# A graph layer on one core: part boundaries moved to groups 200 and 330, nine rounds in place of eight, the second table's fill spread over other groups

## The chip, the cores and the metric

The kernel runs on one core of one Trainium2 chip. The metric is the device time of one execution in microseconds; a kernel's time is the median of its runs. A profiled execution has its own time beside them, and the trace belongs to that execution.

## What is computed

One layer of a graph network over 12,500 nodes with 128 features and 412,500 edges (200,000 drawn ones in both directions and one loop per node), sorted by their end node `dst`; `src` is random within that order. Cut to what matters:

```python
h = x @ Wn + bn;  q = x @ Wq + bq;  k = x @ Wk + bk;  v = x @ Wv + bv
eh = edge_attr @ We + be
hmid   = leaky_relu(concat([q[src], k[dst], eh]) @ A1 + b1, 0.2)
scores = leaky_relu(hmid @ A2 + b2, 0.2)                 # 8 heads
w   = softmax(scores.mean(-1), axis=0)                   # one softmax over all edges
out = segment_sum(w[:, None] * v[dst], src, 12500)
y   = layernorm(h + out) * gamma + beta
result = layernorm(x + y)
```

The sums run over `src`, the edges come sorted by `dst`. So the kernel has to bring 412,500 edge records into another order.

## The kernel before

The weights are folded first: A1 is multiplied into Wq, Wk and We, so that a hidden value of an edge is the sum of a q row, a k row and an edge row. Tables of q and h (by node) and of k and v (by node, each split into three bf16 numbers) are written to DRAM while the first groups already run.

**Groups.** The edges form 403 groups of 1024 (8 tiles of 128). For each group (`make`), `rows` expands the k and v rows of a small window of nodes by one-hot matmuls and adds the edge's part (L931, L936), ScalarE copies them out of PSUM as records of 260 numbers (L946, L947: 128 of k plus edge, 128 of v, 4 times the source's number within its block), and GpSimd scatters them to a table in DRAM, one indirect DMA for each tile (L958). The record of an edge goes to the rows of its block: the nodes are dealt over 98 blocks (source modulo 98), and each block has a fixed stretch of rows in the table. VectorE works out the places: one-hots of the blocks (L851), their count (L862), one-hots of the end nodes (L872), places (L900, L911, L913). PE keeps running counts (L880).

**Parts, tables and rounds.** The 403 groups are cut into parts (`PARTS`). Two tables (`rtab`, TABS = 2) are used in turn, so part 2 writes over the table of part 0. Within a part there are stops: at a stop so many tiles of 128 records are certain to be full in each block (4.4 standard deviations are kept back), and a round works through these tiles of all blocks while later groups still scatter. The last round of a part takes what is left. `Plan` works out the tiles of each part and round from the mean number of records and its spread. Before, with ends 165, 307 and 403, the parts have 15, 13 and 9 tiles a block, and the eight rounds 5, 4, 6, then 4, 4, 5, then 4, 5.

**Units.** A round is cut into units of up to three blocks and 15 tiles (`BLK`, `WIDTH`). A unit loads its tiles (L1150), takes the sources out of them (L1177, or L1179 with a mask in the last round of a part), transposes them (L1187, L1194), writes them as a row to DRAM from ScalarE's queue (`put`, L1199) and reads the row back to all partitions on SP's queue (`spread`, L1204), loads the q rows (L1165), and then goes through its tiles in slices of four: one-hots of the sources (`onehot`, L1216, one instruction for each block that a slice touches), transposed records plus q rows in PSUM (`hidden`, L1230, L1239), leaky relu (L1249 on ScalarE, L1253 on VectorE), scores (L1264), heads (L1290). A running reference takes the place of the softmax's maximum (L1300 to L1320), the weights come from one exponential (L1329), and one-hots times weights (`select` L1338, `weigh` L1352) sum the v halves by node (`add`, L1381). From the second round on the block's earlier sum is loaded from DRAM (L1362), scaled and added (L1397); the sum is stored (L1404).

**The order.** It is written out by hand. `sums_of` gives each unit's operations fixed steps (`lags`; `last_lags` for the last round): units of three slices start every 8 steps, in the last round every 6 steps for three slices and every 8 for four. The main loop emits the groups, six positions for each, and between them the steps. `begun` works out by `PACE` at which group each round begins, and the steps of a round are spread evenly from its beginning to that of the next. After the last group the steps still due before the last round are emitted at once, then the last round and the closing (two layer norms, output). In the closing's first part, during the last round, `rows_x`, `moved` and `put_x` copy x plus beta to a table (L1468 on GpSimd).

**Fills.** Rows of a table that no record may reach must hold zeros before a last round reads them. `fill` gives 49 pieces for each of the first two parts, two blocks each. The first table's are written from an SBUF tile before the first stop, the second table's from a DRAM tile of zeros (DRAM to DRAM). Both go through SP's queue (`fill_piece`, L572) at positions spread evenly between two positions of the main loop; the list is emptied from its end.

```python
n1, n2, n3 = 6 * plan.rounds[0][1], 6 * plan.parts[1][0], 6 * G
until = starts[r] + (starts[r + 1] - starts[r]) * (i - 6 * begun[r]) / (
    6 * (begun[r + 1] - begun[r])
)
```

Of the kernel before, what the change touches and what calls it, by code (L numbers as in the profile page):

```python
# [32 lines left out]
ROWS = 3  # L33
XA = 3
SPAN = 42
PARTS = (74, 127, 165), (225, 278, 307), (367, 403)
NP = len(PARTS)
NR = sum(map(len, PARTS))
PACE = 12
TABS = 2  # L40
WIDTH = 15
BLK = 3
# [7 lines left out]
class Plan:  # L50
# [4 lines left out]
    def __init__(self, n, e, nb, groups):  # L55
        self.n, self.e, self.nb, self.groups = n, e, nb, groups
        at = lambda c: groups * c // 403
        ends = [at(part[-1]) for part in PARTS]
        self.parts = list(zip([0] + ends[:-1], ends))

        def means(g0, g1):
            return [
                (min(e, g1 * GT * P) - g0 * GT * P) * max(0, -(-(n - b) // nb)) / n
                for b in range(nb)
            ]
# [22 lines left out]
        for p, (g0, g1) in enumerate(self.parts):  # L88
            t0 = 0
            for g in map(at, PARTS[p][:-1]):  # L90
                t = int(min(m - 4.4 * m**0.5 for m in means(g0, g)) // P) - t0
# [380 lines left out]
def sorted_path(  # L472
# [76 lines left out]
    zeros = dram.tile([P, fmax, WR], FP, name="zeros")  # L549
# [8 lines left out]
    def fill(k, n):  # L558

        b, top = 0, plan.tiles[k]  # L560
        while b < nb:
            m = 1
            while m < n and b + m < nb and plan.fill[k][b + m] == plan.fill[k][b]:
                m += 1
            a = plan.cap // P - plan.fill[k][b]
            if a < top:
                yield b, m, a, top - a
            b += m

    def fill_piece(k, b, m, a, f, source=None):  # L570
        cap = plan.cap
        piece = nc.sync.dma_start(  # L572
            out=rtab[k][b * cap : (b + m) * cap, :]
            .rearrange("(b c) w -> b c w", b=m)[:, a * P : (a + f) * P, :]
            .rearrange("b (p k) w -> p b (k w)", p=P),
            in_=(empty if source is None else source)[:, :f, :]
            .rearrange("p (o k) w -> p o (k w)", o=1)
            .to_broadcast([P, m, f * WR]),
        ).ins
        if k == 0 and source is None:  # L580
            tc.declare_no_dep(piece, group="rows0.0", reason="rows that no record has reached")
            tc.add_to_no_dep_group("fill0", piece)
# [138 lines left out]
    def spans():  # L721

        lim = const.tile([P, 2], FP)
        for i, (op, most) in enumerate(((ALU.max, SPAN - 1.0), (ALU.min, 0.0))):
            nc.vector.tensor_reduce(lim[:, i : i + 1], mm[:, i, :], AX.X, op)
            sign = 1.0 if op == ALU.max else -1.0
            nc.vector.tensor_scalar(
                bad[:, i : i + 1], lim[:, i : i + 1], sign, -sign * most, op0=ALU.mult, op1=ALU.add
            )
# [24 lines left out]
    def far(name, bufs, **k):  # L754
        return making.enter_context(tc.tile_pool(name=name, bufs=bufs, side="right", **k))
# [307 lines left out]
    units = []  # L1063
# [690 lines left out]
    def later():  # L1754

        for c in range(1, len(chunks)):
            yield from edges(tmp, c, CH // 2)
            yield

    def covered():  # L1760

        most = np_.tile([1, G], FP, name="most")
        g = 0
        while g < G:
            h = g
            while h < G and ready.get(h, ng) == ready.get(g, ng):
                h += 1
            nc.vector.memset(most[:, g:h], float(3 * NB * P * ready.get(g, ng) - P))
            g = h
        nc.vector.tensor_tensor(most, start, most, op=ALU.subtract)  # L1770
        nc.vector.tensor_reduce(bad[0:1, 2 + 2 * NR : 3 + 2 * NR], most, AX.X, ALU.max)

    begun, free_at = [], 0
    for p, (_, g, _, t) in enumerate(plan.rounds):
        free_at = max(free_at, g)
        begun.append(free_at)
        free_at += sum(len(bs) * t + 2.7 for q, bs, _ in units if q == p) / PACE

    with tc.manual_schedule():
        n1, n2, n3 = 6 * plan.rounds[0][1], 6 * plan.parts[1][0], 6 * G  # L1780
        n0 = n1 * 9 // 10
        fills = []
        for k, i0, i1, source in (0, 0, 6 * min(plan.gate, plan.rounds[0][1]) - 12, None), (
            1, n1, n2 - 12, zeros
        ):
            pieces = list(fill(k, 2))
            fills += [
                (i0 + (i1 - i0) * j // len(pieces), (k, *piece, source))
                for j, piece in enumerate(pieces)
            ]  # L1790
        fills = fills[::-1]
        tabs, made, nt = tables(), 0, 1 + (2 * ng - 1) * (NB + 7) + ng
        more, sent, ne = later(), 0, 11 * (len(chunks) - 1)
        done, r = 0, 0
        for i, _ in enumerate(_ for p in range(NP) for _ in make(p)):
            while fills and fills[-1][0] <= i:
                fill_piece(*fills.pop()[1])
            while made < nt and made * n0 < i * nt:
                next(tabs, None)
                made += 1  # L1800
            while sent < ne and sent * n0 < i * ne:
                next(more, None)
                sent += 1
            if i == n1:
                for _ in tabs:
                    pass
                for _ in more:
                    pass
                spans()
                covered()  # L1810
                tab_pool.close()
                steps, starts = sums_of(pool("blk", BLKS))
            if i < n1:
                continue
            while r + 1 < NR and i >= 6 * begun[r + 1]:
                r += 1
            if r + 1 < NR:
                until = starts[r] + (starts[r + 1] - starts[r]) * (i - 6 * begun[r]) / (
                    6 * (begun[r + 1] - begun[r])
                )  # L1820
                while done < until:
                    for fn, args in steps[done]:
                        fn(*args)
                    done += 1
        while done < starts[-1]:
            for fn, args in steps[done]:
                fn(*args)
            done += 1
        making.close()
        for name, of, bufs, k in (  # L1830
            ("blk", "blk2", MORE, {}), ("end", "end", 4, {}), ("gamma", "gam", 1, {}),
            ("row", "row2", ROWS, {}), ("ph", "ph2", 2, dict(space=PSUM)),
            ("turn", "trn", 1, dict(space=PSUM)),
        ):
            late[name] = far(of, bufs, **k)
        for step in steps[done:]:
            for fn, args in step:
                fn(*args)


def kernel(tc, n, n_edges, x, xT, src, dst, dst_g, bounds, xN, *rest):
    nc = tc.nc
    plan = Plan(n, n_edges, x.shape[1], src.shape[1] // GT)
    with tc.tile_pool(name="flag", bufs=1) as fpool:
        flag = fpool.tile([1, 1], I32)
        with ExitStack() as ctx:
            sorted_path(ctx, tc, plan, flag, x, xT, src, dst, dst_g, bounds, xN, *rest)
        other = nc.values_load(flag[0:1, 0:1], min_val=0, max_val=1)  # L1848
        with tc.If(other > 0):
            with ExitStack() as ctx:  # L1850
                general(ctx, tc, n_edges, x, xT, src, dst, *rest)
# [60 lines left out]
```

## Time and profile before

| | |
|---|---|
| median of 3 runs | 4864.8 us (4861.4 to 4865.12) |
| profiled execution, its own time | 4862.14 us |
| its span, first to last instruction | 4860.4 us |
| TensorE clock granted, mean | 0.927 |
| busy share PE / VectorE / ScalarE / GpSimd | 83% / 84% / 64% / 68% |
| first scatter starts, last scatter starts (L958) | 59.0 us, 4310.6 us |

In the rows that follow, PE is TensorE's matmul and PEld its weight load, DVE is VectorE, ACT ScalarE, POOL GpSimd, SP SyncE; a trailing q is that engine's queue of DMA issues and waits. L958 is line 958 of the kernel. A group's row has its line, engine, operation, output and inputs with partitions x elements, the count, then busy us and mean ns of one, then the engine's idle time before it and what ended that idle time. A wait's row has the waiting engine and line, what it waited for, the total, how often, and the longest. The ends of matmuls are modelled, so a busy PE is not a PE at its peak.

### The profile page before, as it was taken

To read this page: it belongs to the slowest core of one execution; us is meant where nothing else is said; L and a number is where in the kernel's file an instruction comes from. 1 tells how busy PE (TensorE), PEld (TensorE's weight loads), DVE (VectorE), ACT (ScalarE), POOL (GpSimd) and SP (SyncE) were. 2 spreads that over 40 slices of the span, in tenths; PEclk is the share of its full clock that TensorE was granted. 3 is DMA by queue.
4 is the path that set the end of the run, shared out by engine and by line. 5 is a ranking of instruction groups with operands and counts; after the bars stand their busy time and mean duration, and the time that the engine had idled before them with its cause. 6 is when DMAs were issued, how large, how long until landed. Compare 5 with 4: busy or idle time off the path is not lost. (4 is left out here: it accounts for less than half of the span.)

```text
span 4860.4 us, 84339 instructions
## 1 busy us (share of the span) xinstructions
PE 4017.1 (83%) x26346; PEld 3094.3 (64%) x26626; DVE 4104.8 (84%) x8629; ACT 3110.9 (64%) x8211; POOL 3305.1 (68%) x3280
## 2 busy tenths in 40 slices
PE   3655665688888899999998888899899999998997
PEld 2434443566766666777676666666677777666776
DVE  8878886698888888889898888898999998977877
ACT  2332222477776667777776666676777777777886
POOL 4777777777777767777777777777777777731103
PEclk7777776799999999999999999999999999999999
DMA  6778876999999998999998888999999999989964
GB/s 197 265 252 266 269 266 214 335 358 346 350 338 346 363 337 307 310 321 313 322 313 311 301 295 301 322 338 321 329 337 329 340 322 322 339 286 329 324 222 162
DMA packets 608627, 1484.42 MB, mean 305 GB/s; under 512 B 101632, under 2 KB 309395, under 8 KB 606374
## 3 DMA queue, kind: packets, MB, share of 16 engines
q1 hardware_dynamic: 445822, 1049.05, 64.5%
q0 software_dynamic: 154752, 429.39, 23.2%
q8 instruction: 211, 3.46, 0.3%
q14 instruction: 250, 2.05, 0.1%
q10 hardware_dynamic: 7592, 0.48, 0.1%
HBM read 906.61 MB, written 611.06 MB: 312 GB/s over the span
## 5 line engine op out<-in xcount | busy, mean ns | idle before, releaser
L958 POOL DMA_INDIRECT rtab<-rec,idx x3224 | 3220.9, 999 | 1087.4 <-issue 775.9
L946 ACT ACTIVATE rec<-pkv 128x1024 f32<-128x1024 f32 x806 | 821.7, 1019 | 1090.4 <-DMA rtab<-rec,idx 557.5
L1352 ACT ACTIVATE ohw<-ohs,w 128x128 f32<-128x128 bf16 x3626 | 1187.0, 399 | 70.8 <-DVE ohs L1338 39.0
L1381 PE MATMUL psm<-rt,ohw 128*128 128x128 f32 x7252 | 1020.6, 284 | 3.0 <-ACT ohw L1352 2.5
L1381 PEld LDWEIGHTS psm<-rt,ohw 128*128 128x128 f32 x7252 | 934.6, 196 | 82.2 <-ACT ohw L1352 21.4
L936 PE MATMUL pkv<-WeS,eat 128*128 128x256 f32 x3224 | 932.3, 416 | 0.0
L1253 DVE TENSOR_TENSOR hm<-ph,hm 128x512 f32<-128x512 f32 (+1 forms) x932 | 625.0, 671 | 294.9 <-ACT hm L1249 292.8
L931 PE MATMUL pkv<-kvs,ohd 128*128 128x256 bf16 x3224 | 534.5, 293 | 325.9 <-ACT rec L946 319.6
L931 PEld LDWEIGHTS <-ohd 128*128 128x128 bf16 x3224 | 319.4, 105 | 581.0 <-issue 461.9
L936 PEld LDWEIGHTS pkv<-WeS,eat 128*128 128x128 f32 x3224 | 612.5, 211 | 72.2
L1230 PE MATMUL ph<-ident,rt 128*128 128x128 f32 x3626 | 581.3, 282 | 76.8 <-DVE hm L1253 74.8
L1230 PEld LDWEIGHTS ph<-ident,rt 128*128 128x128 f32 x3626 | 415.2, 145 | 304.5 <-issue 145.5
L1216 DVE TENSOR_SCALAR ohT<-rowB,iotaP,power 128x512 bf16<-128x512 uint8 (+3 forms) x1176 | 577.2, 509 | 30.1 <-DMA rowB<-row 30.0
L1249 ACT ACTIVATE hm<-ph 128x512 f32<-128x512 f32 (+1 forms) x932 | 532.6, 571 | 61.8 <-PE ph L1239 25.4
L872 DVE TENSOR_SCALAR ohd<-dstb,node 128x1152 bf16<-128x1152 uint8 x404 | 565.0, 1399 | 6.1 <-PE pkv L931 6.1
L1239 PE MATMUL ph<-ohT,qs 128*128 128x512 bf16 (+2 forms) x2072 | 495.3, 329 | 41.1 <-DVE ohT L1216 24.0
L900 DVE TENSOR_TENSOR ats<-pc,oh 128x792 f32<-128x792 f32 x403 | 392.0, 973 | 27.5 <-PE pc L880 27.5
L1264 PE MATMUL psc<-hm,A2s 128*32 128x512 f32 (+2 forms) x1864 | 370.1, 607 | 44.7 <-DVE hm L1253 33.7
L862 DVE TENSOR_REDUCE few<-oh 128x99 bf16<-128x792 bf16 x403 | 395.1, 980 | 13.9
L1338 DVE TENSOR_TENSOR ohs<-iotaE,sl 128x512 bf16<-128x512 bf16 (+1 forms) x932 | 395.2, 424 | 5.0 <-ACT ohw L1352 4.8
L911 DVE TENSOR_REDUCE pos<-ats 128x8 f32<-128x792 f32 x403 | 390.5, 969 | 1.9
L1329 ACT ACTIVATE w<-S,ref 128x12 f32<-128x12 f32 (+2 forms) x280 | 84.7, 302 | 340.6 <-DVE ref L1320 327.7
(193 smaller groups left out, 4072.3 us busy)
## 6 DMA issues: line engine op xcount, KB each, us to landing
rt<-rtab SPq DMA_DIRECT2D x177, 1560.0 KB
rt<-rtab SPq DMA_DIRECT2D x96, 1950.0 KB
eat<-in_ea SPq DMA_DIRECT2D x201, 512.0 KB
rtab<-rec,idx POOLq DMA_INDIRECT x3224
dstb<-dtab SPq DMA_DIRECT2D x201, 256.0 KB
qs<-qtab SPq DMA_DIRECT2D x224, 192.0 KB
atab<-old SPq DMA_DIRECT2D x224, 192.0 KB
rtab<-zeros SPq DMA_DIRECT2D x49, 780.0 KB
```

What stands on the lines that cost most here:

```text
L872: nc.vector.tensor_scalar(to, row[:, cols], node, None, op0=ALU.is_equal)
L931: nc.tensor.matmul(pk[:, i, h, :], ohd[t], kvs, start=(h == 0), stop=False,)
L936: nc.tensor.matmul(pk[:, i, :, :D], eat[:, (j + i) * P : (j + i + 1) * P], WeS, start=False, stop=True,)
L946: nc.scalar.activation(rec[:, :, :, : 2 * D], pk, AF.Copy)
L958: one_tile = nc.gpsimd.indirect_dma_start(out=rtab[p % TABS][:, :], out_offset=bass.IndirectOffsetOnAxis(ap=idxs[g][:, t : t + 1], axis=0) ...
L1216: nc.vector.tensor_scalar(st["oh"][k][:, (a - t0) * P : (b - t0) * P], st["rowB"][:, a * P : b * P], iotaP, power[:, bs[u] : bs[u] + 1], o ...
L1230: nc.tensor.matmul(ph[:, j * P : (j + 1) * P], st["rt"][:, t0 + j, :D], ident, is_transpose=True, start=(j == 0), stop=False,)
L1239: nc.tensor.matmul(ph[:, cols], st["qs"][:, j0 // t, s, :], oh[:, cols], start=False, stop=(s == 1 and j1 == t0 + n),)
L1249: nc.scalar.activation(hm, state[i]["ph", k][:, : n * P], AF.Copy, scale=SLOPE)
L1253: nc.vector.tensor_tensor(hm, ph[:, : n * P], hm, op=ALU.max)
L1352: nc.scalar.activation(ohw[:, j, :], ohs[:, :, j], AF.Copy, scale=st["w"][:, t0 + j : t0 + j + 1])
L1381: nc.tensor.matmul(st["psS"][:, (1 + u) * P : (2 + u) * P], ohw[:, j, :], st["rt"][:, t0 + j, D : 2 * D], start=(k == 0), stop=(k == t - 1),)
```

## The change

Four lines in two places change. The parts get 200, 130 and 73 groups in place of 165, 142 and 96, with stops at 74, 127 and 166 in the first, at 260 and 300 in the second and at 377 in the third: nine rounds in place of eight. The pace by which `begun` is worked out changes, in tiles a group and in the extra counted for a unit. The second table's fill runs from position 60 (group 10) to n2 - 48 (group 192) in place of n1 (group 74) to n2 - 12 (group 163), and since it now overlaps the first table's, the list is sorted by position.

```diff
-PARTS = (74, 127, 165), (225, 278, 307), (367, 403)
+PARTS = (74, 127, 166, 200), (260, 300, 330), (377, 403)
...
-PACE = 12
+PACE = 11.2
...
-        free_at += sum(len(bs) * t + 2.7 for q, bs, _ in units if q == p) / PACE
+        free_at += sum(len(bs) * t + 1.2 for q, bs, _ in units if q == p) / PACE
...
-            1, n1, n2 - 12, zeros
+            1, 60, n2 - 48, zeros
...
-        fills = fills[::-1]
+        fills = sorted(fills, key=lambda piece: piece[0])[::-1]
```

## The prediction

> **What bounds the kernel now.** I read the GpSimd timeline first. From group 0 to group 402 it does one thing, the eight scatters of a group's records (L958):
>
> ```profile
> 2599.79 0.96 POOL L958 DMA_INDIRECT rtab<-rec,idx  x1 [0.30 <-issue]
> 2601.06 0.96 POOL L958 DMA_INDIRECT rtab<-rec,idx  x1 [0.31 <-issue]
> 2602.32 0.96 POOL L958 DMA_INDIRECT rtab<-rec,idx  x1 [0.30 <-DVE ohs L1338]
> ```
>
> One starts every 1.265 us even when it waits for nothing, so a group can't take less than 8 x 1.265 = 10.12 us. Then the windows, cut where rounds begin or end. Columns: stretch and its us, then busy us and (instructions) of PE, PEld, DVE, ACT, POOL, then the granted clock, the DMA share and GB/s.
>
> ```profile
> 499.00:864.00 365.00, 203.45 (x749) 139.63 (x747) 264.03 (x451) 95.78 (x158) 279.39 (x282) 0.71 0.73 245
> 864.00:1577.00 713.00, 608.80 (x4207) 478.35 (x4252) 613.37 (x1228) 485.34 (x1268) 544.38 (x552) 0.95 1.00 350
> 1577.00:1868.00 291.00, 260.39 (x1698) 198.21 (x1717) 248.03 (x524) 199.19 (x554) 205.34 (x208) 0.95 0.96 339
> 1868.00:2462.00 594.00, 544.95 (x3741) 419.86 (x3788) 530.00 (x1120) 424.63 (x1180) 443.90 (x449) 0.98 0.92 316
> 2462.00:3009.00 547.00, 467.30 (x3088) 356.08 (x3122) 466.38 (x942) 359.76 (x980) 417.93 (x424) 0.97 0.88 303
> 3009.00:3496.00 487.00, 441.67 (x2939) 333.25 (x2974) 430.34 (x900) 342.19 (x947) 369.55 (x376) 0.98 0.93 326
> 3496.00:3935.00 439.00, 400.32 (x2909) 325.57 (x2938) 414.37 (x891) 345.03 (x913) 336.29 (x338) 0.97 0.95 334
> 3935.00:4310.00 375.00, 346.15 (x2345) 263.33 (x2372) 332.68 (x714) 275.45 (x768) 281.43 (x287) 0.99 0.94 324
> 4310.00:4398.00 88.00, 77.03 (x502) 55.38 (x509) 55.12 (x153) 55.66 (x171) 5.44 (x4) 0.95 0.86 299
> 4398.00:4717.00 319.00, 295.31 (x2345) 238.35 (x2373) 251.61 (x680) 279.82 (x823) 25.12 (x12) 1.00 0.84 288
> 4717.00:4860.00 143.00, 105.17 (x814) 100.11 (x813) 101.71 (x409) 83.44 (x243) 52.27 (x28) 0.91 0.49 184
> ```
>
> POOL's count over eight is the number of groups. Us for one group, by row: 10.35, 10.33 (713/552 x 8), 11.19, 10.58, 10.32, 10.36, 10.39, 10.45. So up to 4310 us **GpSimd's issue paces the kernel**, some 2 to 4% over its floor, except from 1577 to 2462. Rounds (the work on finished tiles) run under it nearly free until something else fills up: VectorE is at 414.37/439 = 0.944 in the fifth-from-last row (five-tile units), and the DMA engines are at 1.00 between 864 and 1577. After 4310 the scatters are over and what is left runs alone: 88 + 319 + 143 = 550 us, which is the **tail**. Its middle part is the last round:
>
> ```profile
> L1329 ACT ACTIVATE w<-S,ref x41: 298/307/309, 4315.2 to 4717.3; 128x15 f32<-128x15 f32 x32, 128x12 f32<-128x12 f32 x7, 128x8 f32<-128x8 f32 x1, 128x10 f32<-128x10 f32 x1
> ```
>
> 41 units pass their softmax weights (L1329) there, 8 of the round before (3 blocks of 4 tiles) and 33 of the last. From the first of those 33 (at 4398) to the last (4717) are 32 unit times: 319/32 = 9.97 us for 15 tiles.
>
> The slow stretch from 1577 has its cause in the waits of 1411 to 1826:
>
> ```profile
> DVE sl L1177 <- DMA rt<-rtab: 24.3, 12, 5.6
> ```
>
> A unit's tiles come late, just after the stretch in which 350 GB/s filled the DMA engines. The fill of the second table runs from group 74 to 163, that is on top of the rounds.
>
> **What changes in the counts.** By the formulas of Plan the parts have 18, 12 and 7 tiles a block instead of 15, 13 and 9. The sum stays 37, so 3626 tiles are loaded and worked through either way. Rounds by tiles a block: 5, 4, 6 | 4, 4, 5 | 4, 5 before, and 5, 4, 3, 6 | 4, 3, 5 | 3, 4 after. Units grow from 280 to 313: three rounds now have units of 3 blocks x 3 tiles. The last round has 33 units of 12 tiles instead of 15, and `last_lags` spaces them 6 steps apart instead of 8. So 98 tiles leave the tail, and the price is 33 more units under the scatters.
>
> **VectorE's price of a nine-tile unit.** No nine-tile unit is in the trace; I build it from these groups (count, busy us, mean ns):
>
> ```profile
> L1253 DVE TENSOR_TENSOR hm<-ph,hm 128x512 f32<-128x512 f32 x833 | 570.9, 685 | 278.0 <-ACT hm L1249 276.1
> L872 DVE TENSOR_SCALAR ohd<-dstb,node 128x1152 bf16<-128x1152 uint8 x402 | 564.1, 1403 | 6.1 <-PE pkv L931 6.1
> L862 DVE TENSOR_REDUCE few<-oh 128x99 bf16<-128x792 bf16 x403 | 395.1, 980 | 13.9
> L900 DVE TENSOR_TENSOR ats<-pc,oh 128x792 f32<-128x792 f32 x403 | 392.0, 973 | 27.5 <-PE pc L880 27.5
> L911 DVE TENSOR_REDUCE pos<-ats 128x8 f32<-128x792 f32 x403 | 390.5, 969 | 1.9
> L1338 DVE TENSOR_TENSOR ohs<-iotaE,sl 128x512 bf16<-128x512 bf16 x833 | 349.4, 419 | 2.6 <-ACT ohw L1352 2.4
> L1216 DVE TENSOR_SCALAR ohT<-rowB,iotaP,power 128x512 bf16<-128x512 uint8 x589 | 326.8, 555 | 30.1 <-DMA rowB<-row 30.0
> L851 DVE TENSOR_TENSOR oh<-blk,iotaE 128x792 bf16<-128x792 bf16 x403 | 226.9, 563 | 0.0
> ...
> L1216 DVE TENSOR_SCALAR ohT<-rowB,iotaP,power 128x256 bf16<-128x256 uint8 x293 | 113.6, 429 | 0.0
> L1216 DVE TENSOR_SCALAR ohT<-rowB,iotaP,power 128x384 bf16<-128x384 uint8 x195 | 96.5, 495 | 0.0
> ...
> L1253 DVE TENSOR_TENSOR hm<-ph,hm 128x384 f32<-128x384 f32 x96 | 52.8, 550 | 16.8 <-ACT hm L1249 16.7
> L1216 DVE TENSOR_SCALAR ohT<-rowB,iotaP,power 128x128 bf16<-128x128 uint8 x99 | 49.5, 500 | 0.0
> L1338 DVE TENSOR_TENSOR ohs<-iotaE,sl 128x384 bf16<-128x384 bf16 x96 | 45.0, 468 | 2.4 <-ACT ohw L1352 2.4
> ```
>
> Neighbours overlap; in the timeline the one at 3606.92 lasts 0.68 and the next starts after 0.60:
>
> ```profile
> 3606.92 0.68 DVE L1253 TENSOR_TENSOR hm<-ph,hm 128x512 f32<-128x512 f32 x1
> 3607.52 0.96 DVE L911 TENSOR_REDUCE pos<-ats 128x8 f32<-128x792 f32 x1
> ```
>
> So 0.08 us comes off each. A group's own five: 1.403 + 0.980 + 0.973 + 0.969 + 0.563 - 5 x 0.08 = 4.49 us. In the window 3496 to 3935 are 338/8 = 42.25 groups and, by the three-tile slices, 29 units of 15:
>
> ```profile
> L1253 DVE TENSOR_TENSOR hm<-ph,hm 128x512 f32<-128x512 f32 x86 | 58.6, 682 | 10.6 <-ACT hm L1249 10.5
> ...
> L1253 DVE TENSOR_TENSOR hm<-ph,hm 128x384 f32<-128x384 f32 x29 | 16.0, 550 | 3.7 <-ACT hm L1249 3.7
> ```
>
> (414.4 - 42.25 x 4.49)/29 = 7.75 us for a unit of 15, short instructions included. A nine-tile unit is cut into slices of 4, 4 and 1. Its one-hots (L1216, split where a block ends) are 384, 128, 256, 256 and 128 wide: 2.35 us against 2.90 for the six of a 15. Its L1253 are two of 0.685 and a narrow one, about 0.28 by the step from 512 to 384: 1.65 against 2.60. Its L1338 are two of 0.419 and a narrow one that no row has; between 0 and 0.468 I take 0.25: 1.09 against 1.73. Three instructions fewer give 0.24 of overlap back. Sum: 7.75 - 0.55 - 0.95 - 0.64 + 0.24 = **5.85 us**, 0.65 a tile against 0.52.
>
> **Under the scatters, round by round** (`begun` worked out with PACE 11.2 and 1.2 gives the units per group):
> - Groups 300 to 330, 33 units of nine, 1.10 a group: 4.49 + 6.44 = 10.93 us of VectorE a group. Groups 377 to 403, 1.107 a group: 10.97. Both lie over the 10.37 and 10.45 of today. If VectorE were full they cost 17 + 13 = 30 us more; at today's 0.944 they cost 36 + 30 = 66. I take 0.98, since 14.3 of the 24.6 idle us of that window are the two ScalarE waits shown, which vanish behind a full VectorE: 30 x (11.15 - 10.37) + 25.7 x (11.19 - 10.45) = **+42**.
> - Groups 166 to 200, 0.97 units of nine a group: 10.16, at 0.98 10.4, where today's mean is 10.63; I take 10.6, **-1** (-10 to +5).
> - Groups 143 to 166, today 11.19: the second fill (98 blocks x 3 tiles x 133 KB = 39.1 MB) is spread over 182 groups instead of 89, so 0.21 MB a group leave the stretch. To 10.4: 23 x 0.79 = **-18** (-20 to 0).
> - Groups 200 to 260 take the six-tile round that groups 167 to 227 have now: 34 groups go from 10.32 to 10.58, **+9** (0 to +9).
> - Groups 330 to 377, 0.698 units of 15 a group: 9.90, at 0.944 10.49; **+3** (-5 to +5).
> - Groups 10 to 74 get 13.8 MB of the second fill and 7.2 more of the first (98 x 4 tiles, 52.2 MB against 45.0). At 350 GB/s these 21 MB take 60 us of DMA time; the row 499 to 864 alone leaves 27% of 365 us free, and scatters go on at 10.35: **+2** (0 to +8).
>
> Cost under the scatters: 42 - 1 - 18 + 9 + 3 + 2 = **+37** (-35 to +93).
>
> A rule bears on the nine-tile price. The Trainium skill, Perfetto Trace Analysis, Optimizing Scalar/DVE Operations, puts VectorE's fixed overhead per instruction on SBUF at about 60 ns of engine time. By that, two more splits cost 0.12 us; these rows have 2.35 against 9/12 x 3 x 0.555 = 1.25, less two overlaps 0.94 us more. The trace doesn't agree (429 ns at 256 wide, 555 at 512), and I go by the rows; by the rule a unit would be 5.03 us, both stages would need about 10.05, and the 42 would fall away.
>
> **The tail.** 88 us to the first weights of the last round: 8 units of twelve and a gap of 15 steps become 10 units of nine and 8 steps. A unit takes between 5.85 (VectorE) and 7.9 us (63/8, the same step); 7.0 gives 70 + 8 = 78, **-10** (+8 to -22). Then 32 unit times. If all goes with tiles, 12/15 x 9.97 = 7.98. If bytes rule, a unit has 1.60 + 0.59 + 0.20 MB instead of 2.00 + 0.59 + 0.25, and the 13.8 MB of `rows_x` and `put_x` stay (0.42 a unit): 2.81/3.26, so 8.59. These two rows say that bytes rule first and ScalarE later:
>
> ```profile
> 4398.00:4600.00 202.00, 182.86 (x1432) 144.88 (x1450) 162.44 (x419) 170.35 (x500) 25.12 (x12) 1.00 0.94 330
> 4600.00:4717.00 117.00, 112.45 (x916) 93.48 (x925) 89.17 (x262) 109.47 (x324) 0.00 (x0) 1.00 0.66 215
> ```
>
> The middle, 8.28, saves **54** (44 to 64). The closing 143 us lose a shorter last unit, **-2**. Tail: **-66** (-36 to -90).
>
> **Sum.** Profiled execution 4862.1 + 37 - 66 = 4833; the median of the runs is 2.7 above that execution, so **4836 us**; with the bounds of the terms, that case alone runs from 4790 to 4860.
>
> **Rivals.**
> - *The nine-tile units hide.* Their splits cost only the fixed part, GpSimd paces all 403 groups: 4836 - 42 = **4794**. For: scatters still ran at 10.39 with VectorE at 0.944. Against: 10.9 us don't fit in 10.4 by the rows. The skill's rule above would make it so. Chance 0.20.
> - *The round trip of the source row paces nine-tile units: slower.* `put` writes the transposed sources to DRAM, `spread` reads them back, and SP holds everything behind it, loads included, until the row has landed:
>
> ```profile
> SPq L1204 <- DMA row<-slT: 1918.3, 277, 13.0
> ```
>
>   6.9 us a unit. A unit is 8 steps of the order, whatever its tiles: 12 to 15 us now, 0.91 groups = 9.4 us then; tiles must land 5 steps after their load, 5.9 us instead of 7.9. With all 94 nine-tile units before the last scatter at 11.0 us: 33 x 1.57 + 28.4 x 1.56 = 96 in place of 42, sum 4836 + 54 = **4890**. It ends above today's time from a unit time of about 10.6. Against: the last round does 8 steps in 9.97 us. Chance 0.15.
> - *The tail stays with the DMA engines.* 8.59 a unit and no shorter lead-in: it saves 36, and the 37 above eat it: 4836 + 30 = **4866**. For: 0.94 at 330 GB/s. Chance 0.13.
>
> **Chances and range.** A measurement of this kernel tells about 0.2% (9.7 us). My forecast 0.52 and the first rival are faster: 0.72. The third rival is the same: 0.13. The second is slower: 0.15. The range goes from below the first rival to near the second: 4785 to 4885.
>
> **What would show it.** POOL's last scatter at about 4350 us instead of 4311 and some 485 us after it; VectorE above 0.95 in groups 300 to 330 and 377 to 403 with over 11 us a group; groups 143 to 166 near 10.4 and no L1177 waits for tiles there; units of the last round at 8.0 to 8.6 us. I am wrong on the price if those two stages stay at 10.4, and on the cover if VectorE idles there behind L1204's row or late tiles.

## The result, and the profile after

The changed kernel takes 5032.6 us (median of 4 runs, 5023.95 to 5036.18), the kernel before on the same chip 4863.7 us (4 runs): ratio 1.0345, 95% interval 1.0327 to 1.0363. It is slower by 3.5%, where 4836 us was predicted; the time lies outside the range too. The profiled execution has 5023.95 us of its own, a span of 5022.0 us and a mean granted clock of 0.929, hardly another clock than before (0.927).

The windows of the changed kernel, cut where its rounds begin or end (columns as before: stretch and its us, busy us and instructions of PE, PEld, DVE, ACT, POOL, granted clock, DMA share, GB/s):

```profile
864.00:1577.00 713.00, 609.18 (x4269) 480.39 (x4270) 615.02 (x1232) 490.56 (x1284) 544.59 (x550) 0.96 0.95 329
1577.00:1835.00 258.00, 230.34 (x1551) 175.56 (x1549) 222.00 (x472) 177.98 (x497) 183.11 (x187) 0.97 0.97 338
1835.00:2240.00 405.00, 352.53 (x2411) 275.17 (x2409) 345.89 (x827) 273.64 (x769) 268.61 (x272) 0.95 0.91 301
2240.00:2873.00 633.00, 581.95 (x4037) 446.77 (x4038) 566.96 (x1210) 453.00 (x1256) 475.88 (x481) 0.98 0.91 316
2873.00:3299.00 426.00, 387.30 (x2656) 294.07 (x2654) 379.22 (x794) 305.82 (x852) 316.11 (x320) 0.99 0.94 326
3299.00:3688.00 389.00, 337.90 (x2342) 263.97 (x2342) 326.76 (x804) 265.17 (x753) 239.60 (x241) 0.96 0.86 283
3688.00:4179.00 491.00, 443.59 (x3238) 354.97 (x3239) 459.41 (x995) 378.64 (x1005) 370.68 (x376) 0.98 0.96 334
4179.00:4517.00 338.00, 296.29 (x2092) 232.71 (x2090) 281.35 (x709) 238.27 (x675) 206.75 (x208) 0.97 0.84 275
```

The rows from 1835, 3299 and 4179 are the three stages with nine-tile units (groups 166 to 200, 300 to 330, 377 to 403). POOL's count over eight gives the groups: 34, 30.1 and 26, so 11.9, 12.9 and 13.0 us a group, where the other rows of this table stand at 10.4 to 11.0. And in these three **nothing is full**: in the middle one PE is busy for 0.87 of the time, VectorE 0.84, ScalarE 0.68, the DMA engines 0.86, and GpSimd scatters 8 x 1.265 = 10.12 us of every 12.9.

The difference to before, by the starts of the scatters (L958) of the same groups in the two profiled executions, with two later runs that are told of below:

| stretch | before, us | after | e17, old part ends | e18, slices of three |
|---|---|---|---|---|
| start to group 143 | 1577.1 | +2.4 | +3.6 | +3.3 |
| 143 to 166 | 259.0 | -3.8 | -2.4 | -3.9 |
| **166 to 200** | 361.8 | **+43.6** | -1.6 | **+28.3** |
| 200 to 260 | 626.3 | +6.2 | -3.4 | -0.3 |
| 260 to 300 | 411.9 | +14.5 | -0.2 | +19.5 |
| **300 to 330** | 312.9 | **+75.7** | +6.6 | **+53.9** |
| 330 to 377 | 488.4 | +3.2 | -0.1 | -0.3 |
| **377 to last scatter** | 273.2 | **+63.6** | +11.9 | **+52.4** |
| tail, after the start of the last scatter | 549.8 | -43.8 | -9.8 | -44.4 |
| sum | 4860.4 | +161.6 | +4.6 | +108.5 |

The tail gave 44 us, as it should. Under the scatters 205 us were lost, 183 of them in the three nine-tile stages. (The profiled execution of e18 is the slowest of its four runs, 17 us over their median, so its column shows a little less than the median gains.) The waits of 3310 to 3680, inside the middle one (waiting engine and line, what it waited for, total, times, longest):

```profile
ACT w L1329 <- DVE ref L1320: 72.4, 29, 5.9
POOL rtab L958 <- issue: 55.4, 181, 0.6
DVE hm L1253 <- ACT hm L1249: 48.2, 38, 2.1
POOL rtab L958 <- ACT rec L947: 41.8, 20, 4.3
PEld psm L1311 <- DVE mx L1305: 30.9, 18, 3.1
ACT rec L946 <- PE pkv L936: 29.4, 13, 3.4
```

The same groups in the kernel before (3235 to 3548):

```profile
ACT w L1329 <- DVE ref L1320: 30.4, 16, 4.5
DVE hm L1253 <- ACT hm L1249: 17.9, 19, 3.2
PEld psm L1311 <- DVE mx L1305: 11.4, 12, 2.3
```

ScalarE waits for VectorE (72 us of 370, before 30 of 313), VectorE for ScalarE (48, before 18), PE for VectorE (31, before 11), ScalarE for PE (29), and GpSimd at last for ScalarE's records (42). Each has idle time, and each waits for the next; the first three waits were there before and have more than doubled. The timeline shows how one such wait makes another:

```profile
3509.22 0.28 DVE L1319 TENSOR_REDUCE m<-psm 128x1 f32<-128x128 f32 x1
3509.54 0.16 DVE L1320 SCALAR_TENSOR_TENSOR ref<-m,ref 128x1 f32<-128x1 f32 x1
3509.62 0.78 DVE L1216 TENSOR_SCALAR ohT<-rowB,iotaP,power 128x256 bf16<-128x256 uint8 x2
3509.74 0.30 ACT L1329 ACTIVATE w<-S,ref 128x9 f32<-128x9 f32 x1 [1.75 <-DVE ref L1320]
...
3510.13 0.70 PE L1239 MATMUL ph<-ohT,qs 128*128 128x256 bf16 x4 [0.64 <-DVE ohT L1216]
...
3510.16 1.31 ACT L1352 ACTIVATE ohw<-ohs,w 128x128 f32<-128x128 bf16 x4
...
3511.38 1.04 ACT L1278 ACTIVATE z<-psc,b_c 64x512 f32<-64x512 f32 x2
...
3512.44 0.60 ACT L1249 ACTIVATE hm<-ph 128x512 f32<-128x512 f32 x1
...
3513.07 0.69 DVE L1253 TENSOR_TENSOR hm<-ph,hm 128x512 f32<-128x512 f32 x1 [1.80 <-ACT hm L1249]
```

ScalarE stands 1.75 us at L1329 until VectorE has the reference. Behind it in ScalarE's own order are the weighing (L1352), the relu of the scores (L1278) and then L1249, which doesn't need the reference at all: the matmuls that it reads (L1239) had ended by 3510.83 at the latest, and it starts at 3512.44. VectorE's L1253 needs that L1249, and so VectorE stands 1.80 us. The time that VectorE loses so puts off the references after it. This is one passage; the totals above say that it is common (29 times at L1329 and 38 at L1253, in the time of some 31 units).

After the last scatter the same is to be seen without a group beside it. The rows of the lead-in to the last round (what is left of the nine-tile units), and of the last round up to its last weights:

```profile
4517.00:4603.90 86.90, 78.96 (x491) 56.91 (x490) 55.19 (x174) 56.20 (x176) 2.07 (x1) 0.88 0.77 269
4603.90:4880.00 276.10, 265.35 (x1830) 195.52 (x1831) 199.93 (x526) 210.25 (x655) 27.45 (x13) 0.99 0.82 290
```

and the waits of 4517 to 4604:

```profile
ACT w L1329 <- DVE ref L1320: 25.2, 9, 3.8
DVE hm L1253 <- ACT hm L1249: 18.3, 16, 2.7
```

Last scatter 4516.0, first weights of the last round 4607.1: 91 us, where the kernel before needed 87. The weights of the nine-tile units follow one another at 9.1 us there (4513.5 to 4595.1, nine times), with VectorE busy for 0.64 of the row. Last weights at 4883.3: 276.2/32 = 8.63 us a unit in the last round.

### The profile page after: what moved, and what is told of

It is laid out like the page before. It is cut to its first block, busy times and chain, and to the rows that moved or that the text cites. A ratio compares the mean times of both kernels' runs of the same rounds, so it can differ in the third digit from the quotient of the medians.

```text
span 5022.0 us, 87787 instructions
## 1 busy us (share of the span) xinstructions
PE 4157.7 (83%) x27509; PEld 3201.2 (64%) x27509; DVE 4219.1 (84%) x9220; ACT 3194.7 (64%) x8540; POOL 3310.3 (66%) x3281
## 5 line engine op out<-in xcount | busy, mean ns | idle before, releaser
L958 POOL DMA_INDIRECT rtab<-rec,idx x3224 | 3225.7, 1001 | 1287.8 <-issue 780.9
L1352 ACT ACTIVATE ohw<-ohs,w 128x128 f32<-128x128 bf16 x3626 | 1193.5, 399 | 79.2 <-DVE ohs L1338 39.6
L1381 PE MATMUL psm<-rt,ohw 128*128 128x128 f32 x7252 | 1039.9, 285 | 3.6 <-ACT ohw L1352 3.4
L1381 PEld LDWEIGHTS psm<-rt,ohw 128*128 128x128 f32 x7252 | 942.7, 196 | 83.8 <-ACT ohw L1352 11.9
L1253 DVE TENSOR_TENSOR hm<-ph,hm 128x512 f32<-128x512 f32 (+2 forms) x997 | 635.3, 637 | 322.0 <-ACT hm L1249 320.7
L1230 PE MATMUL ph<-ident,rt 128*128 128x128 f32 x3626 | 593.2, 283 | 91.8 <-DVE hm L1253 90.1
L1216 DVE TENSOR_SCALAR ohT<-rowB,iotaP,power 128x512 bf16<-128x512 uint8 (+3 forms) x1371 | 621.4, 476 | 40.9 <-DMA rowB<-row 40.8
L1239 PE MATMUL ph<-ohT,qs 128*128 128x256 bf16 (+3 forms) x2742 | 569.3, 311 | 39.0 <-DVE ohT L1216 37.9
L1249 ACT ACTIVATE hm<-ph 128x512 f32<-128x512 f32 (+2 forms) x997 | 541.7, 543 | 49.8 <-PE ph L1239 23.3
L1264 PE MATMUL psc<-hm,A2s 128*32 128x512 f32 (+3 forms) x1994 | 407.5, 578 | 48.5 <-DVE hm L1253 40.7
L1338 DVE TENSOR_TENSOR ohs<-iotaE,sl 128x512 bf16<-128x512 bf16 (+2 forms) x997 | 424.1, 425 | 1.1 <-ACT ohw L1352 1.1
L1329 ACT ACTIVATE w<-S,ref 128x12 f32<-128x12 f32 (+3 forms) x313 | 94.6, 302 | 499.3 <-DVE ref L1320 487.7
L862 DVE TENSOR_REDUCE few<-oh 128x99 bf16<-128x792 bf16 x403 | 395.1, 980 | 13.9
```

What stands on the lines that cost most here:

```text
L958: one_tile = nc.gpsimd.indirect_dma_start(out=rtab[p % TABS][:, :], out_offset=bass.IndirectOffsetOnAxis(ap=idxs[g][:, t : t + 1], axis=0) ...
L1216: nc.vector.tensor_scalar(st["oh"][k][:, (a - t0) * P : (b - t0) * P], st["rowB"][:, a * P : b * P], iotaP, power[:, bs[u] : bs[u] + 1], o ...
L1230: nc.tensor.matmul(ph[:, j * P : (j + 1) * P], st["rt"][:, t0 + j, :D], ident, is_transpose=True, start=(j == 0), stop=False,)
L1239: nc.tensor.matmul(ph[:, cols], st["qs"][:, j0 // t, s, :], oh[:, cols], start=False, stop=(s == 1 and j1 == t0 + n),)
L1249: nc.scalar.activation(hm, state[i]["ph", k][:, : n * P], AF.Copy, scale=SLOPE)
L1253: nc.vector.tensor_tensor(hm, ph[:, : n * P], hm, op=ALU.max)
```

## The experiments

Theories, as the expectations name them. **V**, the prediction's: VectorE's work sets the nine-tile stages. **S**: a step of the order takes its time (1.47 us), and a unit has eight, whatever its tiles. **U**: a unit has its own chain of some 12 us. **R**: the source row's round trip. **W**: the unit's work passes back and forth between VectorE and ScalarE (and PE), so that all of them idle.

The first sixteen runs fell on chips where the kernel before takes 5799 to 5907 us (the changed kernel's page of one of them, e14, has a clock of 0.867 and 259 GB/s instead of 0.929 and 301); numbers are therefore only compared with the kernel before on the same chip. A nine-tile stage weighs less there, since from group 74 on no stage goes much under 13 us a group in any kernel. Twenty runs of the kernel before on one such chip lie between 5787.7 and 5835.5 us, so where a single run is set against a single run, a difference below some 50 us says little. The last two runs fell on a chip with 4861 us.

**The part ends alone.** The old ends, everything else as changed (new pace, new fill).

```diff
-PARTS = (74, 127, 166, 200), (260, 300, 330), (377, 403)
+PARTS = (74, 127, 165), (225, 278, 307), (367, 403)
```

> The changed kernel with the parts and stops of before, that is, only the pace and the second table's fill are changed. If the whole loss comes with the nine-tile rounds: within 0.3% of the kernel before, and the groups 143 to 166 tell whether the thinner fill speeds them up (the prediction had 18 us) or not.

5786.7 us (8 runs) against 5811.3 (20): 0.9953 [0.9928, 0.9977], where the changed kernel itself, e14 on that chip, has 1.006.

> The changed kernel as it is, on the same chip, as the base of the two doublings. On a chip like the last four: some 50 us above the kernel before, nine-tile stages at 14 to 15 us a group. On a chip that gives 4864 for the kernel before: 5032, within 10, and 11.9 to 13.0 us a group there.

5848.3 us (8 runs): 1.006 [1.0038, 1.0082].

> The changed kernel with the part ends of before, so no unit of nine tiles; the pace and the second fill stay changed. If the nine-tile rounds carry the whole loss, this is level with the kernel before on its chip or up to 0.5% faster (e13_parts_undone was at 0.9953 on another chip): 0.994 to 1.001 of it. If the new pace or the fill carry a share of the loss, it is over 1.005. Where the kernel before takes about 4864 us, groups 143 to 166 tell what the thinner fill is worth without the new rounds: 11.0 to 11.2 us a group before; 10.4 by the prediction, about 11.1 if the fill is not what slows them.

4864.6 us (10 runs) against 4861.1 (13): **1.0004 [0.9989, 1.0020]**. So the new part ends carry the whole loss, and pace and fill together are worth nothing that can be told from zero where the kernel takes 4861 us. In the table the column of e17 is small in every stretch; the +11.9 before the last scatter and the -9.8 of the tail nearly cancel. Groups 143 to 166 took 256.6 us, 11.16 a group, with about half the fill for each group (49 pieces over 182 groups instead of 89): the fill is not the main thing that slows them.

**Slices of three.** Units of nine (and six) tiles are cut 3, 3, 3 instead of 4, 4, 1.

```diff
-return min(4, m), [(j, min(4, m - j)) for j in range(0, m, 4)]
+s = 3 if m in (6, 9) else 4
+return min(s, m), [(j, min(s, m - j)) for j in range(0, m, s)]
...
```

(The same in the two other places where slices of four are cut.)

> The changed kernel with the units of nine tiles cut into slices of 3, 3 and 3 tiles instead of 4, 4 and 1, still in 8 steps. A slice then is one block, so a unit has three one-hots on VectorE instead of five; VectorE's work for a unit falls by about 0.7 us. Theory V: the three stages fall by about 0.7 us a group, the time to about 4965. Theories S, U and R: the steps and the chain are the same, 5024 with up to 15 less.

5805.5 us, +7 on the kernel before (one run).

> The same kernel as in the run with slices of three, on another chip, since the first chip gave the kernel before itself 5799 us and so blurs every stage. On a chip that gives 4864 for the kernel before. Theory V (VectorE's work): the three stages fall by about 0.7 us a group, the time to about 4965. Theories S, U and R: 5024 with up to 15 less. The first chip speaks for more than V: with slices of three the nine-tile stages ran at 13.5 us a group like all others, with the row three steps earlier at 15.9; if it is the slices' shape that counts, all three stages come to 10.4 to 11 and the time to about 4850.

5909.8, +3 (one run).

> Slices of 3, 3 and 3 alone, as twice before, in the hope of a chip on which the kernel before runs at 4864 us. Theory V (VectorE's work, 0.7 us less a unit): the three stages at 12.2 us a group, the time about 4965. Theory S: 5024. If the shape of the slices is the whole cause, as the two slow chips have it (13.4 to 14.2 us a group against 13.2 in the other stages): 10.4 to 11.2 a group, about 4850.

5939.9, +38 (one run). Of these three single runs none tells V from the others.

> The changed kernel as it is, beside the kernel before on the same chip, as the base for the variants, since three chips in a row gave the kernel before 5799 to 5907 us in place of 4864. On such a chip all stages run at about 13.2 us a group; the three nine-tile stages are expected at 15.6 to 16 us a group, as in the run with the row three steps earlier, and the time 150 to 180 us above the kernel before. On a chip that gives 4864: 5032, within 10.

The changed kernel again, beside the next one: 5928.7 (2 runs), 1.0088 [1.0059, 1.0118].

> Slices of 3, 3 and 3 on the same chip. If the shape of the slices is the larger part of the loss: 100 us or more below the changed kernel, within 40 us of the kernel before, the nine-tile stages within 1 us a group of their neighbours. If VectorE's work alone counts (0.7 us a unit): 50 to 60 us below the changed kernel. Theories S, U and R: no more than 15 below.

5903.5 (5 runs), 1.0050 [1.0032, 1.0068].

> Slices of 3, 3 and 3 in nine-tile units, once more beside the kernel before. On a chip that gives 4864 for the kernel before: theory W (the stages pass back and forth between VectorE and ScalarE; this shape takes about 0.7 us of VectorE's and 0.5 us of ScalarE's work from a unit) 1.0 us or more a unit less, the three stages at 10.9 to 11.9 us a group, the time 4900 to 4960; theory V 4965; theory S 5024. On a chip that gives 5800 to 5900 for it: 20 to 40 us above the kernel before.

5909.8 (8 runs), 1.0028 [1.0002, 1.0054].

> The changed kernel with nine-tile units cut into slices of 3, 3 and 3. If the third, one-tile slice carries most of the loss, this is within 0.5% of the kernel before and its nine-tile stages fall below the 11.7 to 13.1 us a group of the changed kernel. If a unit takes its time whatever its slices, stages 300 to 330 and 377 to 403 stay at about 13 us where the kernel before takes about 4864 us, and the whole at 1.02 or more; where the kernel before takes 5800 to 5900 us, 1.003 to 1.007 as in the runs so far.

4953.7 us (4 runs) against 4861.1 (13): **1.0185 [1.0154, 1.0216]**. So 3, 3, 3 takes back about half of the loss (3.45% to 1.85%), and the other half stays with evenly cut units too; that is between the two forecasts. U, and S and R in the form that the expectations give them (same steps, same chain, at most 15 us less), fall with the 79 us between 5032.6 and 4953.7. Windows of the three nine-tile stages of e18:

```profile
1835.00:2225.00 390.00, 332.97 (x2231) 252.61 (x2231) 336.94 (x769) 255.13 (x742) 267.43 (x272) 0.96 0.93 312
3283.00:3650.00 367.00, 315.41 (x2163) 241.32 (x2162) 318.67 (x745) 246.83 (x724) 235.98 (x241) 0.97 0.89 300
4138.00:4464.00 326.00, 282.03 (x1934) 216.62 (x1931) 272.74 (x654) 222.19 (x651) 205.25 (x208) 0.95 0.86 284
```

In groups 300 to 330 VectorE's work falls from 326.76/30.1 = 10.85 us a group to 10.58, and the group from 12.9 to 12.2: less work by 0.27, less time by 0.7. V can't say why, for VectorE's use is only 0.87 here (0.84 before). V's forecast of 4965 us is close to the time by luck: it came from 0.7 us less of VectorE's work for each unit. In the same rows ScalarE's work falls by 0.61 us a group (265.17/30.1 to 246.83/30.1) and PE's by 0.75, so the run doesn't single out one engine. The waits of 3290 to 3640 of e18 (its lines are one higher from L1264 on):

```profile
ACT w L1330 <- DVE ref L1321: 58.4, 28, 4.7
...
POOL rtab L958 <- ACT rec L947: 32.4, 27, 3.9
...
DVE hm L1253 <- ACT hm L1249: 18.3, 30, 2.0
...
DVE sl L1177 <- DMA rt<-rtab: 16.0, 11, 4.0
```

VectorE's wait for L1249 falls from 48 to 18 us, and a new one appears: for a unit's late tiles (L1177) 16.0 us, where the window of the changed kernel has 0.3. So part of what the even slices free is lost again to the loads. Three rows bear on the first, the relu of the scores ahead of it on ScalarE, in the changed kernel two pieces of which the second has one tile, in e18 one:

```profile
L1278 ACT ACTIVATE z<-psc,b_c 64x512 f32<-64x512 f32 x30 | 20.0, 666 | 2.0 <-PE psc L1264 2.0
...
L1278 ACT ACTIVATE z<-psc,b_c 32x128 f32<-32x128 f32 x28 | 10.0, 358 | 0.3
```

```profile
L1279 ACT ACTIVATE z<-psc,b_c 96x384 f32<-96x384 f32 x28 | 15.7, 560 | 0.0
```

1.02 us against 0.56, between a late reference and the L1249 that VectorE waits for. That this piece is the whole of the gain isn't shown; the one-hots (three instead of five) and the matmuls of the scores change too.

**ScalarE's work or VectorE's, doubled.** In nine-tile units one operation is issued twice: L1278 on ScalarE (1.02 us a unit more) or L1338 on VectorE (2 x 0.417 + 0.442 = 1.28 us a unit more, by its rows in the changed kernel, 3310 to 3680):

```profile
L1338 DVE TENSOR_TENSOR ohs<-iotaE,sl 128x512 bf16<-128x512 bf16 x67 | 27.9, 417 | 0.0
...
L1338 DVE TENSOR_TENSOR ohs<-iotaE,sl 128x128 bf16<-128x128 bf16 x27 | 11.9, 442 | 0.0
```

ScalarE's first:

```diff
-for p0, p1, n in pieces:
+for p0, p1, n in pieces * (2 if units[i][2] == 3 else 1):
```

> The changed kernel with one piece of ScalarE's work done twice in units of nine tiles: the relu of the scores (L1278, 1.0 us a unit in two pieces) is written a second time with the same values. Theory W (in the nine-tile stages the loop passes back and forth between VectorE and ScalarE, neither of them full): a large part of it lands on the stages, 0.5 us or more of 1.0 a unit, 45 to 95 us in all 94 units. Theory V (VectorE's work sets the pace): below 15 us, ScalarE is idle a third of the time.

5902.7 us (2 runs): +54 on the changed kernel (e14), that is 0.55 us for each of 99 units. The interval against the kernel before is wide, 1.0071 to 1.0248. Then VectorE's:

```diff
+for _ in range(2 if units[i][2] == 3 else 1):
     nc.vector.tensor_tensor(ohs[:, :, :n], iotaE[:, :, :n],
     ...
```

> The changed kernel with one piece of VectorE's work done twice in units of nine tiles: the one-hots of L1338 (about 1.0 us a unit, three instructions) are written a second time with the same values. Theories V and W: 45 to 95 us more. If only the steps count (S): below 15 us.

5861.4 us (7 runs): +13 on e14, 0.13 us a unit. Against e14's profiled execution, e11's is 57 us longer, with +60 in the three nine-tile stages, and e12's 15 us longer, with +18 there. By V the VectorE work would count in full and ScalarE's not at all; it is rather the other way round. ScalarE, idle for a third of the stage, is on the path, as W has it; but W expected 45 to 95 us from VectorE's work too, and there it missed: 1.28 us more a unit fit almost wholly into VectorE's idle time. On this chip, with its stages at 13 us a group and more, that is only an indication for the other.

**Fewer steps a unit.** Nine-tile units start every six steps instead of every eight.

```diff
-every=max(8, L), lead=turn + 8, sources=-turn - 2 - e, turn=-turn,
+every=6 if plan.rounds[p][3] == 3 else max(8, L), lead=turn + 8, sources=-turn - 2 - e, turn=-turn,
```

> The changed kernel with one thing altered: units of nine tiles start every 6 steps of the order instead of every 8; their instructions, lags and tiles are the same, and each of the three stages then has 5.8 to 6.6 steps a group instead of 7.8 to 8.9. Theory S (a step costs about 1.47 us of time whatever it holds, because instructions that depend on each other stand one step apart on different engines): the stages at groups 166 to 200, 300 to 330 and 377 to 403 fall from 12.0, 13.0 and 13.0 us a group to 10.4 to 11.0, and the time to about 4850 (4830 to 4880). Theory U (a unit's own chain takes 12 us whatever its steps): 5024, within 10. Theory V, that of the prediction's sum (VectorE's work): 5024, the work is the same. Theory R, the prediction's slower rival (the source row's round trip, 8 steps long): falls too, as under S.

5886.5 us, +88 (one run).

> The same kernel as in the run with nine-tile units every 6 steps, on another chip. Theory S (a step costs 1.47 us whatever it holds): the three stages at 10.4 to 11.0 us a group, the time about 4850 (4830 to 4880). Theory U (a unit's chain of 12 us): 5024, within 10. The first chip lies between: 14.7 against 15.9 us a group.

6020.4, +114 (one run).

> Nine-tile units every 6 steps, once more. On a chip that gives 4864 for the kernel before: theory S about 4850 to 4900, the three stages below 11.5 us a group; theory W 5024, within 20, since no work is taken away. On a chip that gives 5800 to 5900 for it: 60 to 115 us above the kernel before, as twice before.

6000.6 (2 runs), 1.0153 [1.0102, 1.0204]. About twice the loss of the changed kernel on such chips (1.006 to 1.009). S expected a gain; the nine-tile stages of the three runs took 14.1 to 15.6 us a group where the changed kernel on such chips (e14, e9) has 13.6 to 14.5. What gets worse is the hold of buffers: SP's loads of tiles (L1150) wait twice as long until the last sums (L1381) of the unit that used the buffer are done. SP's waits over the whole kernel, in the changed kernel (e14), then in e1:

```profile
SPq L1150 <- PE psm L1381: 88.6, 30, 8.5
```

```profile
SPq L1150 <- PE psm L1381: 180.0, 56, 10.4
```

Behind a waiting load SP holds everything else, the groups' loads too. That this is the whole cause wasn't tried.

**More steps a unit, on the kernel before.** The round that begins at the stop of group 278, with units of 12 tiles, gets 11 steps a unit.

```diff
-every=max(8, L), lead=turn + 8, sources=-turn - 2 - e, turn=-turn,
+every=11 if p == 4 else max(8, L), lead=turn + 8, sources=-turn - 2 - e, turn=-turn,
```

> The kernel before, with the units of one round (four tiles a block, groups 278 to 318) started every 11 steps instead of every 8: 9.0 steps a group with no instruction added. Theory S: these 40 groups go from 10.35 to about 13.3 us, the time to about 4980. Theory U: units are as many as before, the time stays at 4864, within 10. Theory V: 4864, the work is the same. Theory R: as S, its 8 steps must last as long.

5822.0 us, +23 (one run), its stage (groups 278 to 318) at 13.9 to 14.0 us a group, where e1, e3 and e4 of that chip have 13.0 to 13.2 in groups 278 to 300. S expected +115 on a chip with 4864 us. Here the run **doesn't decide**: by S the groups would take 9.0 x 1.47 = 13.2 us, which is what that chip's groups take anyhow. What speaks against one fixed price of a step are traces of the other chips: with the same eight steps a nine-tile unit takes 11.8 us in the changed kernel and 11.1 in e18 (12.9/1.10 and 12.2/1.10), and 9.1 where no group runs beside it.

**The source row three steps earlier.**

```diff
-turn = 11 if nk > 3 else 12
+turn = 15 if plan.rounds[p][3] == 3 else 11 if nk > 3 else 12
```

> The changed kernel with the source row of nine-tile units read, transposed, written and read back three steps earlier (and the load three steps earlier with it), so that the round trip has 11 steps until the one-hots instead of 8; all else is the same. Theory R: a unit's time falls from 12 to about 9 to 10 us, the three stages to 11.2 or less, the time to about 4900 or below. Theory S, U and V: 5024, within 15.

5973.4 us, +175 (one run), the slowest of its chip. R expected a gain; a longer lead holds the six record buffers longer, and L1150's wait for L1381 is 182.2 us here. So R isn't refuted by this run alone. Against R speak the waits where the kernel takes 4861 to 5033 us. SP stands at the row for 214.0 of the 370 us of 3310 to 3680, and for 178.4 of the 313 us of the same groups before (3235 to 3548), the same share; VectorE waits for the row only 40.8 us in the whole changed kernel. The changed kernel, SP's row of that window and VectorE's of the whole, then the kernel before:

```profile
SPq L1204 <- DMA row<-slT: 214.0, 32, 8.3
...
DVE ohT L1216 <- DMA rowB<-row: 40.8, 32, 4.9
```

```profile
SPq L1204 <- DMA row<-slT: 178.4, 23, 11.8
```

**Three changes together**: slices of three, every six steps, and the second fill over by group 72.

```diff
...
-            1, 60, n2 - 48, zeros
+            1, 60, n1 - 12, zeros
```

> The changed kernel with three things altered, each read from its own groups: nine-tile units in slices of 3, 3 and 3; the same units every 6 steps instead of 8; the second table's fill over by group 72, before the first round (it ran to group 192). Shape and spacing are read from groups 300 to 330 and 377 to 403 against the run with the slices alone: Theory S expects a clear fall by the spacing, theories U and V none. The fill is read from groups 143 to 166: if the fill made them slow (11.0 to 11.5 us a group in both kernels), they come to 10.4, some 20 us in all; if not, they stay, and groups 10 to 74 show what the earlier fill costs. On a chip that gives 4864 for the kernel before, S and V together: about 4830; V alone: about 4850.

5936.3 us, +34 (one run). Groups 143 to 166 took 13.40 us each, where e14 and e13 have 13.24 and 13.44: with no fill at all in that stretch it is no faster. The early fill cost groups 10 to 74 nothing there (12.14 us each; e9 and e10 have 12.07 and 12.17).

No run is faster than both kernels wherever it ran: the old part ends with the new pace and fill gain 0.5% on one chip and nothing on the other.

## Why the prediction was wrong

**The cover: VectorE's use of 0.98. This step failed.** "I take 0.98, since 14.3 of the 24.6 idle us of that window are the two ScalarE waits shown, which vanish behind a full VectorE." They didn't vanish, they grew: L1253's waits for L1249 went from 14.3 us in 439 to 48.2 in 370, and they are one half of the loop that the timeline shows. The prediction's own sign for a wrong cover, VectorE idle behind L1204's row or late tiles, was not it: late tiles cost VectorE 0.3 us of that window and the row none. VectorE's use fell from 0.944 to 0.84 and 0.83, and the two stages cost 76 + 64 = 139 us instead of 42. Both bounds of that term (30 and 66; the -35 of the sum takes it at nothing, as the first rival does) assumed a use no lower than in the row of 15-tile units; the use was the unknown, and nothing bounded it from below. The row that it was taken from had 29 units in 42 groups, 0.69 a group, and already left VectorE idle for 0.056 of the time; the nine-tile stages have 1.1 units a group.

**The price itself was right.** VectorE's work: predicted 10.93, 10.97 and 10.16 us a group for the three stages, measured 326.76/30.1 = 10.85, 281.35/26 = 10.82 and 345.89/34 = 10.17. That the parts add up so well is partly luck: the narrow L1338 was too low (0.25 taken, 0.442 in the row above) and the two one-hots of 128 (L1216) too high (0.500 each taken, 0.361 measured in 3310 to 3680).

The rule of the Trainium skill, Perfetto Trace Analysis, Optimizing Scalar/DVE Operations, by which a unit would be 5.03 us, isn't borne out: by it the stage's VectorE work would be near 10.05 us a group, an estimate from the page's 60 ns, where the window has 10.85.

**Groups 166 to 200** were taken as -1, since 10.16 us of VectorE lie under the 10.6 of today: +44. It is the same step: with 0.97 units of nine a group the use went to 345.89/405 = 0.85. Likewise groups 260 to 300, which weren't given a term (0.82 units of twelve a group): +14.5, at a use of 0.89. It can't be the one-tile slice there, for e18 has +19.5.

**The unit's time.** The lead-in to the last round was to have units of 5.85 to 7.9 us, "7.0". With the groups gone and VectorE at 0.64 they took 9.1. A nine-tile unit that runs without groups doesn't go by its VectorE work either; the lead-in gave +4 instead of -10. The upper end was counted wrongly. In the kernel before, the first and the last of the eight units of that stretch pass their weights at

```profile
4315.19 0.30 ACT L1329 ACTIVATE w<-S,ref 128x12 f32<-128x12 f32 x1 [4.01 <-DVE ref L1320]
...
4378.32 0.30 ACT L1329 ACTIVATE w<-S,ref 128x8 f32<-128x8 f32 x1 [0.93 <-DVE ref L1320]
```

and these 63 us are seven intervals, not eight: 9.0 us a unit in eight steps, with 12 tiles (the last has 8) as with nine. In e18 the lead-in has 90.5 us (4463.5 to 4554.0): even slices bring nothing there.

**Groups 143 to 166**: -18 by 0.21 MB a group less fill; it came to -4, and -2.4 in e17. The DMA share of the stretch before did fall, from 1.00 to 0.95, and the L1177 waits of 1411 to 1826 only from 24.3 to 20.5 us. The full DMA engines and the late tiles were seen rightly; that they paced the stretch was a step too far. What paces it isn't settled: L1329 waits in 1580 to 1835 for 30.1 us before and 34.1 in e17.

Of the signs that were named, the last scatter came at 4516 instead of 4350, 506 us after it instead of 485, and VectorE at 0.84 instead of above 0.95, with the foretold "over 11 us a group" going on to 12.9.

**Right**: the early fill (+2 predicted, +2.4 with everything before group 143); groups 200 to 260 (+9, measured +6); 330 to 377 (+3, +3); the closing (-2, -4); the last round (8.28 a unit predicted, 8.59 as its upper bound, measured 8.63: -43 instead of -54; what sets it isn't shown: the DMA engines are at 0.82 in that row, ScalarE at 0.76, PE at 0.96 with its modelled ends). The tail as a whole: -44 instead of -66, within its bounds.

**The rivals.** The nine-tile units didn't hide. The third rival's tail is the one that came: 8.59 a unit and no shorter lead-in, measured 8.63 and 91 us instead of 87. By its own words it saves 32 x (9.97 - 8.59) = 44 us, not 36, and 44 is what the tail gave; its total failed by the stages under the scatters, which it took over. The second one had the sign and the nearest picture: "a unit is 8 steps of the order, whatever its tiles", 11.0 us a unit; it was 12.9/1.10 = 11.8. Its cause, the row's round trip, shows in no wait that grew; its price was worked out for the two later stages. In the first, 11.0 us a unit would have been 0.97 x 11.0 = 10.7 a group, no loss to speak of; a unit took 11.92/0.97 = 12.3 there.

**What is left open.** Half of the loss goes with the 4, 4, 1 cut (e18). For the other half the runs speak against VectorE's work alone (e12, and the use of 0.87 in e18) and against one fixed price of a step. That VectorE, ScalarE and PE wait for one another is shown; that ScalarE's time counts in part is shown by e11 only where the kernel takes 5800 us and more; which handover sets the 11.1 us of an evenly cut unit (12.2/1.10) is open. PE is a candidate, busy at 0.91 in the lead-in, but its rows include modelled ends, and no run changed its work alone; the late tiles of e18 (16 us of 350) are another. Giving L1249 a place ahead of the late L1329 in ScalarE's order wasn't tried.

## What to carry to other kernels

An engine's work divided by an assumed use gives a stage's time no better than that use is known: where units pass between several in-order engines, take the use from a row with as many units for each group, and when the change makes units denser than any row, let it fall further in the bounds. Before a busy engine is trusted to swallow the waits, look who causes them: a wait on an engine whose own order puts unrelated work behind a late value comes back as idle time of the engine that it waited for. When units get smaller, count what each unit brings regardless of its size, and price the odd last slice by itself.

## What the runs showed that was not expected

The granted clock hardly differs between the two executions, and the engines' busy time by 3 to 4% (VectorE 4105 and 4219 us, PE 4017 and 4158), and yet three stages take 12 to 24% longer (44 of 362, 76 of 313, 64 of 273 us) with no engine and no DMA share above 0.91. Chips differ more than kernels here: the same changed kernel takes 5032.6 us on one and 5848.3 and 5928.7 on two others; why isn't shown. On those two its loss is only 0.6 and 0.9% instead of 3.5%, so a small difference measured there says little about its size on the first; what the even slices take back could first be measured in e18.
